# Scatters of a graph convolution released in groups of three chunks, and later one by one, by TensorE's progress

## The chip, the core and the metric

The kernel runs on one core of a Trainium2 chip. A core has TensorE (PE in the profile, its weight loads PEld), VectorE (DVE), ScalarE (ACT), GpSimd (POOL) and SyncE (SP), each with a queue that it works through in order; 16 DMA engines move data. The metric is the device time of one execution in microseconds (us). The kernel before takes 5031.5 us, the median of 3 runs (5031.15 to 5031.81).

## The reference

A layer of a graph network: 12500 nodes with 128 features, 412500 edges. Each edge takes a row of the normalised node table at `dst`, multiplies it with a filter made from its 20 attributes, and adds it to the row of `src`.

```python
h = jnp.maximum(_layernorm(x, axis=-1), 0.0)
h = h @ W_in2f
Wij = ssp(f_ij @ W_f1 + b_f1) @ W_f2 + b_f2      # ssp(x) = softplus(x) - log 2
Wij = Wij * rcut_ij[:, None]
x_ij = h[idx_j] * Wij                            # idx_j = dst, sorted
agg = jax.ops.segment_sum(x_ij, idx_i, num_segments=12500)   # idx_i = src, not sorted
out = x + ssp(agg @ W_o1 + b_o1) @ W_o2 + b_o2
```

## The kernel before

The edges are cut into 806 **chunks** of 512 (`CH`), a chunk into four **tiles** of 128 edges (`QT = 4`). `step(k)` (L1053) is called once for each chunk and writes out, in the order in which the engines are to work, what several chunks need at that moment; the schedule is manual, so each engine's queue is the order of the calls.

In step k TensorE does, in this order: the second half of the filter for chunk k+1 (`value`, tile `v`, L834), the rows of the node table for chunk k+2, selected by a one-hot product (`pick`, tile `picked`, L846), the count of places already taken for a later chunk (`rank`, tile `free`, L799 and L766), then for every second chunk the first half of the filter (`hidden`, tile `z`, L710). ScalarE scales `picked` to `hg` (L856) and sets up the next `v` (L826); VectorE reduces `free` to `top` (L771), from which come the places (`slot`), and multiplies `v` with `hg` to the messages `o` (`message`, L864).

Messages are summed in two stages. First each row of a message is written to a place of its own in a table `slots` in HBM, sorted by blocks of 128 nodes: this is the **scatter** (`Group.scatter`, L867), an indirect DMA on POOL's queue for each of the four tiles (L873, 128 rows of 516 bytes), so 3224 in all. Later, when all chunks of a segment of the edges are written, `Collect` reads the table back (`m`), makes one-hot matrices on VectorE (`to`, L932) and adds up on TensorE (`add`, tiles `acc` and `numbers`, L953). There are seven segments (`SEGS`, in groups of four chunks); the first has 352 chunks, so until chunk 369 (352 and `DELAY` = 17) TensorE has no collecting to do, and behind that the adds of a finished segment run at the end of each step, beside the chunks of the next.

Which order holds the scatters: a message is put on the list `waiting`, and the inner function `scatter` of `step` (L1072) takes chunks from it. From chunk 24 (`PACED`) on, and until 12 steps before the end, it does so at one point of step k alone: behind `value` of chunk k+1. It then issues the four scatters of chunk k-1, and the first of them is made to wait for the last matmul of that `v` (a semaphore of TensorE; "pace of TensorE"). The other three have no wait for TensorE. Every scatter waits for the landing of the scatter eight before it, and the first of a chunk for VectorE's message. In the other direction, `behind` (L595) makes matmuls wait for scatters 16 chunks back, and the buffers of `o` are 16 chunks deep (`BACK`).

```python
                if k + 1 not in vs:
                    vs[k + 1] = g.value(c, bs.pop(k + 1))
                    scatter(k, kept["v"])
```

Of the kernel before, what the change touches and what calls it, by code (L numbers as in the profile page):

```python
# [45 lines left out]
def gnn_kernel(  # L46
# [498 lines left out]
    with tc.tile_pool(name="edge", bufs=2) as edge, tc.tile_pool(  # L545
# [57 lines left out]
        class Group:  # L603
# [101 lines left out]
            def hidden(self, c):  # L705

                z = psum.tile([P, 2, CH], F32, name="z")
                for k in range(2):
                    rows = slice(32 * (c + k), 32 * (c + k) + RBF)
                    mm = nc.tensor.matmul(z[:, k, :], wf1[rows, :], self.f[rows, :],  # L710
                                          start=True, stop=True)
                    if k == 1:
                        behind(mm, self.g * NCHUNK + c - LZ, 3)
                self.pair[c] = z

            def hidden_log(self, c):
# [36 lines left out]
            def rank(self, c):  # L753

                seg = self.seg
                if c == 0:
                    self.top = edge.tile([P, TG], F32, name="top")
                    self.slot = edge.tile([P, TG], I32, name="slot", bufs=8)
                k = self.g * NCHUNK + c
                if k > seg.c0:  # L760
                    self.pass_on()
                if k == seg.cleared and k > seg.c0:
                    used = self.used()
                    self.limit(6 * len(segs), ALU.is_gt, seg.low, used[:, :, :NBLK - 1])
                    self.limit(6 * len(segs) + 1, ALU.is_gt, seg.low_last, used[:, :, NBLK - 1:])
                nc.tensor.matmul(free, after, self.inb[c], start=k == seg.c0, stop=False,  # L766
                                 skip_group_check=True)
                kept["inb"] = self.inb[c]

            def rank_end(self, c):  # L770
# [58 lines left out]
            def value(self, c, v):  # L829

                r = self.pair[c // 2 * 2][:, c % 2, :]
                k = self.g * NCHUNK + c - 1
                for i in range(QT):
                    mm = nc.tensor.matmul(v[:, i, :], r[:, i * P:(i + 1) * P], wf2,  # L834
                                          start=False, stop=True, skip_group_check=True)
                    if i == 1:
                        behind(mm, k, k % 2)
                kept["v"] = mm
                return v

            def pick(self, c, at, ps):
# [3 lines left out]
                for i in range(QT):  # L845
                    mm = nc.tensor.matmul(ps[:, i, :], at[:, i * P:(i + 1) * P], near,  # L846
                                          start=i == 0, stop=i == QT - 1, skip_group_check=True)
                    if i == 1:
                        behind(mm, k, 2 + k % 2)

            def picked(self, c, ps):

# [11 lines left out]
                nc.vector.tensor_mul(o[:, :, :P], v, hg)  # L864
                self.o[c] = o

            def scatter(self, c, after=None):  # L867

                views = self.seg.views
                o = self.o.pop(c)  # L870
                for i in range(QT):
                    j = c * QT + i
                    put = nc.gpsimd.indirect_dma_start(  # L873
                        out=views[j % VIEWS],
# [2 lines left out]
                        in_offset=None,  # L877
                    )
                    puts.append(put.ins.name)
                    if i == 0 and after is not None:  # L880
                        tc.add_manual_dep(
                            put.ins, after.ins.name,
                            mybir.DependencyInfo(mybir.DependencyClass.Sync,
# [10 lines left out]
        class Collect:  # L894
# [47 lines left out]
            def add(self, u):  # L942
                b0, nb, t0, nt = self.units[u]
                m, to = self.m.pop(u), self.to.pop(u)
                for j in range(nb * nt):
# [7 lines left out]
                    nc.tensor.matmul(self.acc[b // few][:, i, :], m[:, j, :P], to[:, j, :],  # L953
                                     start=t == 0, stop=t == self.seg.tiles(b) - 1)
# [94 lines left out]
        tops, ps = [], {}  # L1049
        waiting = []  # L1050
        LAG, PACED = 1, 24

        def step(k, units=()):  # L1053

# [11 lines left out]
            def message(k):  # L1066
                g, c = of(k)
                g.message(c, vs.pop(k), hgs.pop(k))
                waiting.append(k)
                scatter(k)  # L1070

            def scatter(k, after=None):  # L1072
                while waiting and (waiting[0] < PACED or k >= NCH - PACED // 2
                                   or after is not None and waiting[0] <= k - LAG):
                    j = waiting.pop(0)
                    g, c = of(j)
                    g.scatter(c, after if j >= PACED and k < NCH - PACED // 2 else None)

            if k in vs:
                message(k)  # L1080
# [369 lines left out]
```

## Time and profile before

| | |
|---|---|
| median of 3 runs | 5031.5 us |
| the profiled execution: time, span of its instructions | 5066.41 us, 5064.7 us |
| busy: PE, PEld, DVE, ACT, POOL | 3601.4, 2760.7, 3149.0, 2793.9, 3135.5 us |
| mean granted clock of TensorE | 0.784 |
| scatters (L873) | 3224, mean 959 ns each |

The profiled execution is 0.7% longer than the median of the others. No engine is busy for more than 71% of the span. "Granted clock" is the share of TensorE's clock that the throttle let through. In the trace's rows an idle time stands in brackets with what ended it: "issue" is a wait for nothing that the profile shows, "remote" one whose end came from a semaphore that it could not put down to an instruction. Of a scatter the trace shows how long POOL works on it (about 0.96 us); between two scatters that wait for nothing POOL always shows 0.30 us.

### The profile page before, as it was taken

To read this page: it belongs to the slowest core of one execution; us is meant where nothing else is said; L and a number is where in the kernel's file an instruction comes from. 1 tells how busy PE (TensorE), PEld (TensorE's weight loads), DVE (VectorE), ACT (ScalarE), POOL (GpSimd) and SP (SyncE) were. 2 spreads that over 40 slices of the span, in tenths; PEclk is the share of its full clock that TensorE was granted. 3 is DMA by queue.
4 is the path that set the end of the run, shared out by engine and by line. 5 is a ranking of instruction groups with operands and counts; after the bars stand their busy time and mean duration, and the time that the engine had idled before them with its cause. 6 is when DMAs were issued, how large, how long until landed. Compare 5 with 4: busy or idle time off the path is not lost. (4 is left out here: it accounts for less than half of the span.)

```text
span 5064.7 us, 68387 instructions
## 1 busy us (share of the span) xinstructions
PE 3601.4 (71%) x21594; PEld 2760.7 (55%) x21594; DVE 3149.0 (62%) x7192; ACT 2793.9 (55%) x5494; POOL 3135.5 (62%) x3298
## 2 busy tenths in 40 slices
PE   5666666566655565567777887887777787787778
PEld 3444444344433344356666666666666666666667
DVE  5565555555544454556666666666666676677767
ACT  5556566565555555555555555555555555555533
POOL 5566666666666666666666666666656666666553
PEclk7666666766666666679999888888988888888889
DMA  4555545445433334446657655567656765665658
GB/s 140 171 160 164 171 138 174 147 134 160 130 99 114 113 113 141 131 154 199 190 189 238 187 178 185 175 192 230 188 169 185 219 207 168 183 216 163 186 144 229
DMA packets 494767, 858.10 MB, mean 169 GB/s; under 512 B 141018, under 2 KB 276558, under 8 KB 494398
## 3 DMA queue, kind: packets, MB, share of 16 engines
q1 hardware_dynamic: 390798, 640.38, 42.3%
q0 software_dynamic: 103168, 213.15, 12.5%
q8 instruction: 174, 2.85, 0.2%
q14 instruction: 195, 1.60, 0.1%
q10 hardware_dynamic: 432, 0.13, 0.0%
HBM read 457.62 MB, written 395.69 MB: 168 GB/s over the span
## 5 line engine op out<-in xcount | busy, mean ns | idle before, releaser
L873 POOL DMA_INDIRECT slots<-o,slot x3224 | 3090.8, 959 | 1831.2 <-issue 808.9
L856 ACT ACTIVATE hg<-picked,rcut 128x128 f32<-128x128 f32 x3224 | 913.3, 366 | 1243.5 <-remote 356.7
L834 PEld LDWEIGHTS v<-wf,r 128*128 128x128 f32 x6448 | 1067.2, 247 | 324.2 <-issue 214.8
L834 PE MATMUL v<-wf,r 128*128 128x128 f32 x6448 | 1153.8, 335 | 73.4 <-issue 36.5
L864 DVE TENSOR_TENSOR o<-v,hg 128x512 f32<-128x512 f32 x806 | 553.0, 686 | 698.4 <-remote 207.0
L953 PEld LDWEIGHTS acc<-to,m 128*128 128x128 f32 x5660 | 782.1, 219 | 281.0 <-issue 144.0
L953 PE MATMUL acc<-to,m 128*128 128x128 f32 x5660 | 836.6, 308 | 117.1 <-DVE agg L987 45.2
L710 PE MATMUL z<-f,wf 20*128 20x512 f32 x1612 | 605.7, 826 | 355.7 <-issue 185.6
L771 DVE TENSOR_REDUCE top<-free 128x4 f32<-128x392 f32 x806 | 449.1, 557 | 602.2 <-remote 341.9
L932 DVE TENSOR_TENSOR to<-numbers,m 128x640 f32<-128x640 f32 (+3 forms) x793 | 630.4, 825 | 40.0 <-remote 12.0
L719 ACT ACTIVATE a<-z,bf 128x1024 f32<-128x1024 f32 x402 | 445.7, 1109 | 379.4 <-PE v L834 113.6
L747 DVE TENSOR_TENSOR inb<-numbers,blk 128x392 f16<-128x392 f32 x806 | 447.7, 556 | 297.3 <-PE picked L846 73.9
L846 PE MATMUL picked<-near,at 126*128 126x128 bf16 x3224 | 393.6, 248 | 330.2 <-issue 193.5
L799 PE MATMUL free<-inb,rest_of 128*128 128x392 f16 x806 | 318.1, 395 | 420.9 <-issue 277.2
L742 DVE SCALAR_TENSOR_TENSOR r<-z,nbf,a 128x1024 f32<-128x1024 f32 x402 | 513.5, 1277 | 127.9 <-ACT a L722 64.0
L826 ACT ACTIVATE v<-bf 128x512 f32<-128x512 f32 x806 | 486.6, 604 | 180.7 <-DVE o L864 72.5
L846 PEld LDWEIGHTS <-at 126*128 126x128 bf16 x3224 | 302.7, 114 | 389.7 <-issue 364.5
L953 PE MATMUL numbers<-to,m 128*128 128x128 f32 x2492 | 398.7, 324 | 121.0 <-DVE to L932 87.6
L953 PEld LDWEIGHTS numbers<-to,m 128*128 128x128 f32 x2492 | 367.5, 233 | 213.6 <-DVE to L932 136.6
L722 ACT ACTIVATE a<-a,half 128x1024 f32<-128x1024 f32 x402 | 461.5, 1148 | 13.1
L710 PEld LDWEIGHTS z<-f,wf 20*128 20x128 f32 x1612 | 152.4, 226 | 551.7 <-issue 303.0
L720 ACT ACTIVATE a<-a 128x1024 f32<-128x1024 f32 x402 | 424.9, 1057 | 12.8
(126 smaller groups left out, 1845.0 us busy)
## 6 DMA issues: line engine op xcount, KB each, us to landing
m<-slots SPq DMA_DIRECT2D x307, 387.0 KB
rel<-rel_d SPq DMA_DIRECT2D x202, 504.0 KB
m<-slots SPq DMA_DIRECT2D x278, 322.5 KB
f<-in_f_t SPq DMA_DIRECT2D x101, 512.0 KB
slots<-o,slot POOLq DMA_INDIRECT x3224
m<-slots SPq DMA_DIRECT2D x193, 258.0 KB
slots<-zero SPq DMA_DIRECT2D x96, 387.0 KB
slots<-zero SPq DMA_DIRECT2D x58, 516.0 KB
```

Of the source, the lines that this page charges most:

```text
L710: mm = nc.tensor.matmul(z[:, k, :], wf1[rows, :], self.f[rows, :], start=True, stop=True)
L722: nc.scalar.activation(a, a, AF.Ln, bias=half, scale=0.5)
L742: nc.vector.scalar_tensor_tensor(r, z, nbf1, a, op0=ALU.max, op1=ALU.add)
L771: nc.vector.tensor_reduce(self.top[:, c * QT:(c + 1) * QT], free_v, axis=mybir.AxisListType.X, op=ALU.max)
L826: nc.scalar.activation(v, spread(bf12, QT), AF.Copy)
L834: mm = nc.tensor.matmul(v[:, i, :], r[:, i * P:(i + 1) * P], wf2, start=False, stop=True, skip_group_check=True)
L846: mm = nc.tensor.matmul(ps[:, i, :], at[:, i * P:(i + 1) * P], near, start=i == 0, stop=i == QT - 1, skip_group_check=True)
L856: nc.scalar.activation(hg[:, i, :], ps[:, i, :], AF.Copy, scale=self.rcut[:, j:j + 1])
L864: nc.vector.tensor_mul(o[:, :, :P], v, hg)
L873: put = nc.gpsimd.indirect_dma_start(out=views[j % VIEWS], out_offset=bass.IndirectOffsetOnAxis(ap=self.slot[:, j:j + 1], axis=0), in_=o[: ...
L932: nc.vector.tensor_tensor(to[:, :n, :], count_ps[:, None, :].to_broadcast([P, n, P]), m[:, :n, P:].to_broadcast([P, n, P]), op=ALU.is_equal)
L953: nc.tensor.matmul(self.acc[b // few][:, i, :], m[:, j, :P], to[:, j, :], start=t == 0, stop=t == self.seg.tiles(b) - 1)
```

## The change

Instructions, their order on each engine and all buffers stay. What changes is for which matmul which scatter waits.

- `kept["mm"]` now holds TensorE's latest matmul, whichever it is, at each point of the program.
- The inner `scatter` is called at four points of a step: behind `value` ("v"), `pick` ("pick"), `rank` ("rank"), and at the step's end, behind `hidden` and the adds ("end").
- Chunks 24 to 368 (`j < LONE`, 352 + 17): only at "v", and only when three whole chunks are waiting. Their 12 scatters are issued together, and the first alone waits for TensorE: chunks j, j+1 and j+2 for `v` of chunk j+4. 
- Chunks 369 and up, until 12 steps before the end: at each of the four points one scatter, which waits for the latest matmul. So of chunk k-1 the first scatter waits for `v` of chunk k+1 as before, the second for `picked` of chunk k+2, the third for `free`, the fourth for the last add or `z` of step k.
- `Group.scatter` takes the tiles to be issued as an argument.

```diff
-            def scatter(self, c, after=None):
+            def scatter(self, c, tiles, after=None):
 
                 views = self.seg.views
-                o = self.o.pop(c)
-                for i in range(QT):
+                o = self.o[c] if tiles[-1] < QT - 1 else self.o.pop(c)
+                for i in tiles:
...
-                    if i == 0 and after is not None:
+                    if i == tiles[0] and after is not None:
...
+        LONE = segs[0].c1 + DELAY
...
-                waiting.append(k)
+                waiting.append((k, 0))
                 scatter(k)
 
-            def scatter(k, after=None):
-                while waiting and (waiting[0] < PACED or k >= NCH - PACED // 2
-                                   or after is not None and waiting[0] <= k - LAG):
-                    j = waiting.pop(0)
-                    g, c = of(j)
-                    g.scatter(c, after if j >= PACED and k < NCH - PACED // 2 else None)
+            def scatter(k, point=None):
+                while waiting:
+                    j, i = waiting[0]
+                    if j < PACED or k >= NCH - PACED // 2:
+                        n, after = QT - i, None
+                    else:
+                        where, n = ("v", 3 * QT) if j < LONE else ("each", 1)
+                        if point not in (("v", "pick", "rank", "end") if where == "each" else (where,)):
+                            return
+                        if j * QT + i + n > (k - LAG + 1) * QT:
+                            return
+                        after = kept["mm"]
+                    while n > 0:
+                        j, i = waiting.pop(0)
+                        g, c = of(j)
+                        e = min(QT, i + n)
+                        g.scatter(c, range(i, e), after)
+                        after = None
+                        n -= e - i
+                    if e < QT:
+                        waiting.insert(0, (j, e))
+                        return
...
-                    scatter(k, kept["v"])
+                    scatter(k, "v")
...
                 g.pick(c, ats.pop(k + 2), ps[k + 2])
+                scatter(k, "pick")
...
                 next(r, None)
                 tops.append(r)
+            scatter(k, "rank")
...
                     summed[0].add(summed[1])
                 summed[:] = c, u
+            scatter(k, "end")
```

POOL's queue in the first part, before: the four scatters of chunk 61, those of chunk 62, and the first of chunk 63. `PE_49` in the brackets is a wait for TensorE, `DVE_49` one for VectorE, `DMASW` one for an earlier scatter's landing; the numbers are those of buffers.

```order
L873 DMA slots0_116<-o_3273,slot_2930 206848x129 [waits DMASW4_49,DVE_49,PE_49]
L873 DMA slots0_116<-o_3273,slot_2930 206848x129 [waits DMASW5_49]
L873 DMA slots0_116<-o_3273,slot_2930 206848x129 [waits DMASW6_49]
L873 DMA slots0_116<-o_3273,slot_2930 206848x129 [waits DMASW7_49]
L873 DMA slots0_116<-o_3312,slot_2930 206848x129 [waits DMASW0_49,DVE_49,PE_49]
L873 DMA slots0_116<-o_3312,slot_2930 206848x129 [waits DMASW1_49]
L873 DMA slots0_116<-o_3312,slot_2930 206848x129 [waits DMASW2_49]
L873 DMA slots0_116<-o_3312,slot_2930 206848x129 [waits DMASW3_49]
L873 DMA slots0_116<-o_3353,slot_2930 206848x129 [waits DMASW4_49,DVE_49,PE_49]
```

The same place of POOL's queue in the changed kernel.

```order
L875 DMA slots0_116<-o_3273,slot_2930 206848x129 [waits DMASW4_49,DVE_49]
L875 DMA slots0_116<-o_3273,slot_2930 206848x129 [waits DMASW5_49]
L875 DMA slots0_116<-o_3273,slot_2930 206848x129 [waits DMASW6_49]
L875 DMA slots0_116<-o_3273,slot_2930 206848x129 [waits DMASW7_49]
L875 DMA slots0_116<-o_3308,slot_2930 206848x129 [waits DMASW0_49,DVE_49]
L875 DMA slots0_116<-o_3308,slot_2930 206848x129 [waits DMASW1_49]
L875 DMA slots0_116<-o_3308,slot_2930 206848x129 [waits DMASW2_49]
L875 DMA slots0_116<-o_3308,slot_2930 206848x129 [waits DMASW3_49]
L875 DMA slots0_116<-o_3345,slot_2930 206848x129 [waits DMASW4_49,DVE_49,PE_49]
```

Two of three waits for TensorE are gone; the scatters of a group of three chunks stand behind one.

POOL's queue in the second part, before: chunk 501, and the first scatter of chunk 502.

```order
L873 DMA slots1_117<-o_23643,slot_23303 116992x129 [waits DMASW4_49,DVE_49,PE_49]
L873 DMA slots1_117<-o_23643,slot_23303 116992x129 [waits DMASW5_49]
L873 DMA slots1_117<-o_23643,slot_23303 116992x129 [waits DMASW6_49]
L873 DMA slots1_117<-o_23643,slot_23303 116992x129 [waits DMASW7_49]
L873 DMA slots1_117<-o_23698,slot_23303 116992x129 [waits DMASW0_49,DVE_49,PE_49]
```

And there in the changed kernel.

```order
L875 DMA slots1_117<-o_23643,slot_23301 116992x129 [waits DMASW4_49,DVE_49,PE_49]
L875 DMA slots1_117<-o_23643,slot_23301 116992x129 [waits DMASW5_49,PE_49]
L875 DMA slots1_117<-o_23643,slot_23301 116992x129 [waits DMASW6_49,PE_49]
L875 DMA slots1_117<-o_23643,slot_23301 116992x129 [waits DMASW7_49,PE_49]
L875 DMA slots1_117<-o_23698,slot_23301 116992x129 [waits DMASW0_49,DVE_49,PE_49]
```

Every scatter now waits for TensorE, three more waits for each chunk, and nothing else moves.

TensorE's queue in a step of the second part, in the changed kernel (before, the rows are the same but for their line numbers, which are one or two lower): the four points lie behind `v`, behind the last `picked`, behind the second `free`, and behind the `acc`.

```order
L835 MATMUL v<-wf_63,r 128x128 x4
L847 LDWEIGHTS at
L847 MATMUL picked<-near,at 128x128
...
L800 LDWEIGHTS rest_of
L800 MATMUL free<-inb,rest_of 128x392
L767 LDWEIGHTS after
L767 MATMUL free<-inb,after 128x392
L710 MATMUL z<-f,wf_62 128x512 x2
L955 MATMUL acc<-to,m 128x128 x10
L835 MATMUL v<-wf_63,r 128x128 x4
```

Nothing moved here; the rows show where on TensorE the four points are.

More of the change, by code (lines that the diff above doesn't have):

```diff
@@ L713, in hidden @@
                         behind(mm, self.g * NCHUNK + c - LZ, 3)
+                kept["mm"] = mm
                 self.pair[c] = z
@@ L765, in rank @@
                     self.limit(6 * len(segs) + 1, ALU.is_gt, seg.low_last, used[:, :, NBLK - 1:])
-                nc.tensor.matmul(free, after, self.inb[c], start=k == seg.c0, stop=False,
-                                 skip_group_check=True)
+                kept["mm"] = nc.tensor.matmul(free, after, self.inb[c], start=k == seg.c0,
+                                              stop=False, skip_group_check=True)
                 kept["inb"] = self.inb[c]
@@ L837, in value @@
                         behind(mm, k, k % 2)
-                kept["v"] = mm
+                kept["mm"] = mm
                 return v
@@ L849, in pick @@
                         behind(mm, k, 2 + k % 2)
+                kept["mm"] = mm
             def picked(self, c, ps):
@@ L952, in add @@
                         self.acc[b // few] = self.room(b // few)
-                    nc.tensor.matmul(self.acc[b // few][:, i, :], m[:, j, :P], to[:, j, :],
-                                     start=t == 0, stop=t == self.seg.tiles(b) - 1)
+                    kept["mm"] = nc.tensor.matmul(
+                        self.acc[b // few][:, i, :], m[:, j, :P], to[:, j, :],
+                        start=t == 0, stop=t == self.seg.tiles(b) - 1)
                     if t == self.seg.tiles(b) - 1 and (i == few - 1 or b == NBLK - 1):
```

## The prediction

> **What bounds the kernel now.** I read the page first, then busy times by stage, then rows of POOL, TensorE and VectorE one under the other. The page:
>
> ```profile
> span 5064.7 us, 68387 instructions
> PE 3601.4 (71%) x21594; PEld 2760.7 (55%) x21594; DVE 3149.0 (62%) x7192; ACT 2793.9 (55%) x5494; POOL 3135.5 (62%) x3298
> PEclk7666666766666666679999888888988888888889
> L873 POOL DMA_INDIRECT slots<-o,slot x3224 | 3090.8, 959 | 1831.2 <-issue 808.9
> ```
>
> No engine is full, so the time goes in waits. The stages are cut at 178, 2211 and 4828 us, where chunks 24 and 369 and the unpaced end begin; the columns are the stretch, busy us and count for PE, PEld, DVE, ACT and POOL, then granted clock, DMA share, GB/s. Below them are the messages that fall into the two stages.
>
> ```profile
> 178.00:2211.00 2033.00, 1237.87 (x5779) 836.26 (x5778) 1090.36 (x2782) 1188.51 (x2354) 1316.83 (x1373) 0.66 0.45 141
> 2211.00:4828.00 2617.00, 2068.90 (x13975) 1685.83 (x13973) 1794.92 (x3802) 1424.57 (x2807) 1625.23 (x1697) 0.87 0.62 192
> ...
> L864 DVE TENSOR_TENSOR o<-v,hg x345: 672/691/693, 182.5 to 2209.9; 128x512 f32<-128x512 f32 x173
> ...
> L864 DVE TENSOR_TENSOR o<-v,hg x424: 674/683/695, 2212.6 to 4826.9; 128x512 f32<-128x512 f32 x142
> ```
>
> A chunk takes 2033 / 345 = 5.89 us in the first stage and 2617 / 424 = 6.17 us in the second. POOL's four scatters take 4 x (0.96 + 0.30) = 5.04 us of either, so POOL is nearest to full, and idles 0.85 and 1.13 us for each chunk. Why it idles is seen in one group of the first stage: POOL's first, last and next scatter, TensorE's matmuls in between, and VectorE's reduction that waits for `free`.
>
> ```profile
> 1260.80 0.97 POOL L873 DMA_INDIRECT slots<-o,slot  x1 [2.77 <-PE free L766]
> ...
> 1274.73 0.96 POOL L873 DMA_INDIRECT slots<-o,slot  x1 [0.30 <-issue]
> 1278.21 0.95 POOL L873 DMA_INDIRECT slots<-o,slot  x1 [2.52 <-remote]
> ...
> 1268.87 0.53 PE L766 MATMUL free<-inb,after 128*128 128x392 f16 x1
> 1269.20 1.33 PE L834 MATMUL v<-wf,r 128*128 128x128 f32 x8
> 1278.50 0.48 PE L799 MATMUL free<-inb,rest_of 128*128 128x392 f16 x1 [7.58 <-DVE top L771]
> ...
> 1277.88 0.57 DVE L771 TENSOR_REDUCE top<-free 128x4 f32<-128x392 f32 x1 [7.39 <-remote]
> ```
>
> `free` ended at 1269.40, yet VectorE starts on it at 1277.88; `v` ended at 1270.53, yet POOL's next scatter starts at 1278.21. Both come a good two us after POOL's last scatter ended (1275.69). So **TensorE's announcements do not get through while POOL scatters back to back**: they are let go when POOL has stopped. VectorE, ScalarE and TensorE stand still for seven us, and POOL itself then waits for a `v` that is long done. The same in the second stage, with runs of four and of eight scatters (first, last, next), and TensorE's rows beside the run of four:
>
> ```profile
> 2988.39 0.96 POOL L873 DMA_INDIRECT slots<-o,slot  x1 [2.67 <-PE picked L846]
> ...
> 2992.18 0.96 POOL L873 DMA_INDIRECT slots<-o,slot  x1 [0.30 <-issue]
> 2994.37 0.96 POOL L873 DMA_INDIRECT slots<-o,slot  x1 [1.23 <-PE acc L953]
> ...
> 2844.71 0.96 POOL L873 DMA_INDIRECT slots<-o,slot  x1 [2.10 <-PE free L766]
> ...
> 2853.56 0.96 POOL L873 DMA_INDIRECT slots<-o,slot  x1 [0.30 <-issue]
> 2856.71 0.96 POOL L873 DMA_INDIRECT slots<-o,slot  x1 [2.19 <-PE free L766]
> ...
> 2989.66 1.38 PE L953 MATMUL acc<-to,m 128*128 128x128 f32 x10
> 2990.88 1.06 PE L834 MATMUL v<-wf,r 128*128 128x128 f32 x8
> 2991.77 0.39 PE L846 MATMUL picked<-near,at 126*128 126x128 bf16 x4
> 2992.16 0.33 PE L766 MATMUL free<-inb,after 128*128 128x392 f16 x1
> ```
>
> From one run's start to the next: 5.98 us for 4, 12.00 for 8, 17.41 for 12 scatters, so 1.50, 1.50 and 1.45 us a scatter. The pause grows with the run (1.23, 2.19, 2.52); length hardly matters. A chunk costs 5.8 to 6.0 us in this way as long as `v` is done in time, and the kernel stands close above it: 5.89 and 6.17.
>
> What lies above it in the second stage are pauses in which `v` truly comes late:
>
> ```profile
> 2928.31 0.95 POOL L873 DMA_INDIRECT slots<-o,slot  x1 [0.31 <-issue]
> 2932.36 0.96 POOL L873 DMA_INDIRECT slots<-o,slot  x1 [3.09 <-PE picked L846]
> ...
> 2927.44 2.93 PE L953 MATMUL acc<-to,m 128*128 128x128 f32 x12
> 2930.16 1.92 PE L834 MATMUL v<-wf,r 128*128 128x128 f32 x8
> 2932.36 0.33 PE L766 MATMUL free<-inb,after 128*128 128x392 f16 x1
> ```
>
> **First stage, chunks 24 to 368.** The change takes 230 of 345 waits for TensorE off POOL, so runs of 12 become the rule; before, they stand among runs of 4 and 8. The price of a group is read where two runs of 12 follow each other:
>
> ```profile
> 1451.19 0.96 POOL L873 DMA_INDIRECT slots<-o,slot  x1 [2.46 <-PE picked L846]
> ...
> 1468.59 0.95 POOL L873 DMA_INDIRECT slots<-o,slot  x1 [2.54 <-PE v L834]
> ...
> 1486.43 0.96 POOL L873 DMA_INDIRECT slots<-o,slot  x1 [2.99 <-PE v L834]
> ```
>
> Two groups in 35.24 us, 17.6 each. 115 groups x 17.6 = 2024 us against 2033: a gain of 9 us, if the awaited `v` is ready when POOL stops. It should be: the last `v` of the run at 1260.80 had ended 5.2 us before POOL did. That the scatters come up to two chunks later delays nobody: the matmuls that wait for scatters wait for those 16 chunks back, over 90 us at 5.89 a chunk. The two waits taken away per group cost nothing in themselves: POOL's 0.30 us stands before scatters with and without.
>
> TensorE will stand still in every group for seven us, as at 1278.50. The clock granted in this stage is 0.66 already; were it 0.50 throughout, TensorE's 1237.87 / 345 = 3.59 us of work a chunk would become 4.74, and 14.2 for three, still under 17.6. The Trainium skill (TensorE: Matmul & The Clock Gate, "Why this matters for your kernels") says the same against this stage: idle gaps of more than about 3 us drop the clock to half. By it TensorE would be cold for most of each group, and the sum stays as above, since 14.2 is under 17.6; the row of 0.66 agrees with it.
>
> **Second stage, chunks 369 to 792.** Each scatter gets a wait, three more for each chunk, 1272 in all. A wait that is already met costs nothing (the 0.30 us again; every scatter's landing wait is of this kind). One that is not met costs a pause. Behind it on POOL's queue are only more scatters, and for those nobody waits for 16 chunks; VectorE, ScalarE and TensorE feel POOL only through the held announcements. What a single scatter holds back no row shows, since all runs are of 4, 8 or 12. From below: nothing, 1.26 us from one to the next; from above: as long as a run of four does, 0.96 + 1.23 = 2.19 us. I take the 1.5 us a scatter that 4 and 8 agree on, being nearest.
>
> The four points are not spread evenly: in the step at 2989.66 the adds end at 2991.04, `v` at 2991.94, `picked` at 2992.16, `free` at 2992.49, four points in 1.45 us. So once one scatter has run, the waits of the next three are mostly met, and the four go as they do today, one scatter shifted: the last of a chunk goes at the end of the adds, ahead of `v`. Where `v` is late that is a gain: the adds of the late step ended at 2930.37, 1.71 us before `v` at 2932.08, so one scatter (1.26 us) fits into what was pause. All of today's excess is 6.17 - 6.00 = 0.17 us a chunk. One scatter in four leaves the pause, so about a quarter to a third of it goes: 0.05 us x 424 = 21 us. From above the gain is bounded by 0.17 x 424 = 72 us, unless TensorE itself gets faster (third rival).
>
> Ahead of chunk 24 and in the last 237 us nothing changes. Sum: -9 - 21 = -30 us on the profiled execution's 5066.41, 0.6%; on the median of 5031.5 that is 5001 us.
>
> **Rivals.** *A second pause in each step (slower).* The scatter that goes at the end of the adds holds back `v`, `picked` and `free` in their turn, POOL has run out of met waits, and pauses before the next three. Price: at 1.50 us for a run of one, 0.24 us more than the 1.26 of today's back-to-back scatters, and up to 0.93 (1.23 - 0.30) if it holds as long as a run of four; 0.4 us in half of the steps is 85 us, less 9 of the first stage: 5107. It decides when the added pauses exceed the 0.05 us saved, that is, when more than about one step in eight has one. For it: the four points span 1.45 us, about as long as one scatter holds. Against it: a POOL that falls behind finds all its waits met.
>
> *`v` late in the first stage (slower).* With no pause at 4 or 8, TensorE gets its answers later, and a `v` that misses the release costs what the late one above cost, 3.09 - 1.23 = 1.86 us. In one group of three that is 38 x 1.86 = 71 us, and the time about 5080. Against it: 5.2 us of reserve.
>
> *TensorE freed (much faster).* If no announcement is held longer than one scatter, VectorE and ScalarE answer at once, and the second stage goes at 1.45 us a scatter, 5.80 a chunk: 0.37 x 424 = 157 us and 9: 4865.
>
> *No effect.* Runs of 4 and 8 form again out of met waits, and the first stage stays as it is: 5031. The Trainium skill speaks for this: SBUF — State Buffer, "SBUF: two separate sides", has it that a DMA and a compute instruction cannot slow each other, but for GpSimd and VectorE at their shared port. By it when scatters go would not matter to TensorE at all. The row of `top` at 1277.88 speaks against it.
>
> **How the numbers follow.** Forecast 0.38 (5001, its own range 4960 to 5025), second pause 0.26 (5107), late `v` 0.10 (5080), TensorE freed 0.14 (4865), no effect 0.12 (5031). 0.2%, or 10 us, is what can be told from no change. Faster: 0.36 of the forecast and 0.14; within 0.2%: 0.12 and the forecast's last 0.02; slower: 0.26 and 0.10. The range reaches from 4900, which leaves out most of the freed case, to 5120, which leaves out those second pauses that cost more than 0.4 us in half of the steps.
>
> **What would show it.** In the first stage POOL's rows should show a pause after every 12 scatters and at no other place, of 2.5 to 3 us, and the next run 17.4 to 17.8 us after the last; pauses over 3.5 us mean that `v` is late. The second stage is decided by its length (2617 us now) and by runs shorter than four: single scatters with pauses on both sides, and a stage longer than 2617, mean the second pause. The freed case would show in waits of `hg` and `top` for TensorE that shrink, and in a granted clock above 0.87. Wrong in both directions would be the forecast if single scatters hold announcements far shorter or longer than 1.5 us.

## The result and the profile after

The kernel takes 5050.05 us after the change (5045.73 to 5055.21, 5 runs) against 5031.15 before (5026.58 to 5031.81, 5 runs): a ratio of 1.0041 with a 95% interval of 1.0028 to 1.0054, 19 us slower. 5001 was forecast. The profiled execution of after took 5052.65 us. Its page:

```profile
span 5050.9 us, 69659 instructions
PE 3592.7 (71%) x21594; PEld 2756.4 (55%) x21594; DVE 3158.7 (63%) x7192; ACT 2787.6 (55%) x5494; POOL 3145.6 (62%) x3298
PEclk7666666666666666668899898889888988888879
L875 POOL DMA_INDIRECT slots<-o,slot x3224 | 3100.7, 962 | 1797.2 <-issue 778.8
```

No engine's busy time has grown by more than 10 us, and none is full. The stages, cut again where chunks 24 and 369 and the unpaced end begin (after, busy times by stretch):

```profile
173.00:2223.00 2050.00, 1235.86 (x5776) 834.82 (x5776) 1092.39 (x2781) 1185.30 (x2349) 1315.13 (x1368) 0.66 0.45 139
2223.00:4803.00 2580.00, 2054.93 (x13971) 1677.98 (x13969) 1801.60 (x3800) 1419.76 (x2809) 1635.61 (x1702) 0.88 0.64 195
```

The first stage takes 2050 us where the profile before showed 2033 and the forecast said 2024; the second 2580, where 2617 stood and 2596 was forecast. So the first stage lost time and the second gained some. Two groups of the first stage, one clean and one not (after, POOL's first and last scatter of each group, and the first of the group behind):

```profile
841.17 0.96 POOL L875 DMA_INDIRECT slots<-o,slot  x1 [2.69 <-remote]
...
855.08 0.96 POOL L875 DMA_INDIRECT slots<-o,slot  x1 [0.31 <-issue]
858.63 0.97 POOL L875 DMA_INDIRECT slots<-o,slot  x1 [2.59 <-remote]
...
872.57 0.96 POOL L875 DMA_INDIRECT slots<-o,slot  x1 [0.30 <-issue]
880.32 0.96 POOL L875 DMA_INDIRECT slots<-o,slot  x1 [6.79 <-PE v L835]
```

The first group costs 17.46 us, as priced; the second 21.69, since POOL stops at 873.53 and then waits 6.79 us for `v`. TensorE, ScalarE and one row of VectorE in that group, after:

```profile
866.37 0.53 PE L767 MATMUL free<-inb,after 128*128 128x392 f16 x1
866.70 1.91 PE L373 MATMUL hps<-win,xT 128*128 128x128 f32 x8
868.41 1.09 PE L835 MATMUL v<-wf,r 128*128 128x128 f32 x8
...
873.59 2.08 PE L710 MATMUL z<-f,wf 20*128 20x512 f32 x4 [0.78 <-issue]
877.96 2.08 PE L835 MATMUL v<-wf,r 128*128 128x128 f32 x8 [2.29 <-ACT v L827]
```

```profile
871.38 0.57 DVE L772 TENSOR_REDUCE top<-free 128x4 f32<-128x392 f32 x1 [4.76 <-issue]
...
875.64 0.60 ACT L375 ACTIVATE hb<-hps 128x512 bf16<-128x512 f32 x1 [5.92 <-PE z L710]
876.14 1.14 ACT L858 ACTIVATE hg<-picked,rcut 128x128 f32<-128x128 f32 x4
877.31 0.60 ACT L827 ACTIVATE v<-bf 128x512 f32<-128x512 f32 x1
```

`hps` (rows of the node table that TensorE makes in between) ended at 868.61, but ScalarE stands idle for 5.92 us and starts on it at 875.64, 2.1 us after POOL stopped. Behind it in ScalarE's queue are `hg` and the start of the next `v`; so the `v` that POOL waits for begins only at 877.96. This announcement was held to the end of the run, and what POOL waits for depends on it: the release comes first, and then a chain of 4.4 us more. The trace's own records of TensorE's semaphore show the release: none between 865.84 and 875.62, then six within 0.28 us.

Not every announcement is held that long. `free` ended at 866.90, and VectorE took it up at 871.38, 4.5 us late but with POOL in the middle of its run. In the profile before, 55 of the 94 times that VectorE stood idle for over half a microsecond ahead of `top` in the first stage ended like this, while POOL was still scattering, and 65 of 67 in the second. So the sentence of the prediction that announcements do not get through while POOL scatters back to back is too strong: they come through microseconds late, some within the run and the rest behind it.

Over all 114 groups of the first stage the awaited `v` ended after POOL had stopped in 36; the pause is 2.55 us in the median and over 3.2 us in 18. In each of these 18 POOL starts again 0.28 us after `v` has ended, so it is `v` that it waits for. The cycle of a group is 17.45 us in the median and 17.88 in the mean: 0.43 x 114, some 50 us, lies in the late ones.

In the second stage shorter runs have appeared, as meant (after, first scatter of each of several runs):

```profile
2271.13 0.96 POOL L875 DMA_INDIRECT slots<-o,slot  x1 [1.54 <-PE picked L847]
...
2279.93 0.96 POOL L875 DMA_INDIRECT slots<-o,slot  x1 [1.51 <-PE numbers L955]
...
2283.01 1.06 POOL L875 DMA_INDIRECT slots<-o,slot  x1 [0.86 <-PE free L767]
...
2292.57 0.96 POOL L875 DMA_INDIRECT slots<-o,slot  x1 [0.70 <-PE acc L955]
2294.95 0.96 POOL L875 DMA_INDIRECT slots<-o,slot  x1 [1.42 <-PE picked L847]
```

A run of six takes 8.80 us here, and the lone scatter at 2292.57 holds POOL for 2.38 us up to the next one. Over the stage runs of 4, 5, 7 and 8 cost 6.00, 7.40, 10.42 and 11.85 us in the median, 1.48 to 1.50 a scatter; only 25 scatters of 1696 stand alone, at 2.00 us in the mean.

### The profile page after: what moved, and what is told of

It reads as the page before. It is cut to its first block, busy times and chain, and to the rows that moved or that the text cites. A ratio compares the mean times of both kernels' runs of the same rounds, so it can differ in the third digit from the quotient of the medians.

```text
span 5050.9 us, 69659 instructions
## 1 busy us (share of the span) xinstructions
PE 3592.7 (71%) x21594; PEld 2756.4 (55%) x21594; DVE 3158.7 (63%) x7192; ACT 2787.6 (55%) x5494; POOL 3145.6 (62%) x3298
## 5 line engine op out<-in xcount | busy, mean ns | idle before, releaser
L955 PEld LDWEIGHTS acc<-to,m 128*128 128x128 f32 x5660 | 794.5, 221 | 291.2 <-issue 168.4
L955 PE MATMUL acc<-to,m 128*128 128x128 f32 x5660 | 850.5, 311 | 127.8 <-issue 51.4
```

Of the source, the lines that this page charges most:

```text
L955: kept["mm"] = nc.tensor.matmul(self.acc[b // few][:, i, :], m[:, j, :P], to[:, j, :], start=t == 0, stop=t == self.seg.tiles(b) - 1)
```

## The experiments

**Two kinds of chip.** The runs come from several chips (which one the first comparison used is not on record), and they fall into two kinds: in five comparisons, the first among them, the kernel before takes 5026 to 5072 us, and in three, on three chips, 4202 to 4209 us. Ratios and differences are always to the kernel before on the same chip. The theory at the start: the first part (three chunks behind one `v`) loses through late `v`, the second (a wait at each scatter) gains a little. The rival: the first part gains, and the single waits of the second part lose. The first part alone, as a change of after:

```diff
-                        where, n = ("v", 3 * QT) if j < LONE else ("each", 1)
+                        where, n = ("v", 3 * QT) if j < LONE else ("v", QT)
```

> Only the groups of three chunks up to chunk 368; behind that the scatters of a chunk wait for v as before. Theory (late v in the first stage): 15 to 25 us slower than before, first stage about 2049 us as in the changed kernel. Rival (the second stage's single waits cost it): 5 to 10 us faster than before.

The second part alone:

```diff
-                        where, n = ("v", 3 * QT) if j < LONE else ("each", 1)
+                        where, n = ("v", QT) if j < LONE else ("each", 1)
```

> Only the single waits behind chunk 368; up to there the scatters of a chunk wait for v as before. Theory (late v in the first stage): within 10 us of before or up to 30 us faster. Rival (a second pause in each step): 20 to 30 us slower than before, with many runs of one scatter.

With them the kernel before was profiled twice more:

> The kernel before, for a second profile, since the one shown took 5066.41 us and its median 5031. If the profiled execution was an odd one, its second stage (chunks 369 to 792, 2617 us there) comes out some 30 us shorter here and its first stage (2033 us) the same; the first part of the change then loses and the second gains little or nothing. If 2617 us is typical, the second part of the change gains 36 us, and something of equal size must be lost where no profile shows it.

> The kernel before once more, for a third profile: as before_again.

The four ran on a chip where the kernel before takes 4202.3 us (21 runs). First part alone: 4203.04 us, ratio 1.0000 (0.9991 to 1.0009). Second part alone: 4201.13, ratio 0.9998 (0.9989 to 1.0007). The kernel before took 4207.68 and 4203.72 under the profile. The first part's result is neither theory's; the second's lies within the 10 us of its theory, but so does no effect at all. The kernel before had become 16% shorter in its first stage and 18% in its second, so nothing on its odd profile could be told from it. So the whole change was run on another such chip, with the first part again, and with a measurement of what bounds that kernel: in before, every second chunk's last scatter issued twice.

> The changed kernel, unaltered, beside the kernel before on the same chip. The first two experiments came from a chip on which the kernel before takes 4202 us and TensorE's announcements are not held while POOL scatters. Theory: the change can only act where they are held. If the kernel before takes about 4200 us here as well, the changed kernel takes the same, within 5 us; if it takes about 5030 us, the changed kernel is 10 to 30 us slower, as in the first comparison. Rival (the change acts through something else, such as the 1272 added waits on POOL): slower by 10 to 30 us on either kind of chip.

> The first stage's part of the change alone (three chunks of scatters behind one v), beside the whole change on the same chip. If announcements are held here (the kernel before at about 5030 us): theory, the first stage gives back its 17 us through late v, so 10 to 20 us slower than before, and some 30 of 115 pauses over 3.2 us; rival, the first stage saves its 9 us and what was lost lies in the second stage and the tail, so 5 to 15 us faster. If they are not held (4200 us): within 5 us of before.

```diff
+                    if i == QT - 1 and (self.g * NCHUNK + c) % 2 == 0 and 24 < self.g * NCHUNK + c < 793:
+                        put = nc.gpsimd.indirect_dma_start(
...
                     puts.append(put.ins.name)
```

> The kernel before with the last scatter of every second chunk from 26 on issued twice (same rows, same addresses, 384 scatters more), so that the price of one scatter is measured by itself. Where announcements are held, theory: each costs what a run costs a scatter, 1.45 to 1.50 us, so 557 to 576 us more; rival (POOL's own time sets the pace): 1.26 us each, 485 us more. Where they are not held, both say 1.26 us each or a little less, 450 to 485 us, if POOL is the bound there; less than 300 us if it is not.

The whole change: 4201.11 us against 4202.1, ratio 0.9998 (0.9989 to 1.0008). The first part: 4200.26, ratio 0.9996 (0.9987 to 1.0005). Lines of the whole change's page and its stages on this chip (the third row is VectorE's copy that waits for a buffer of `o`):

```profile
span 4200.0 us, 69659 instructions
L858 ACT ACTIVATE hg<-picked,rcut 128x128 f32<-128x128 f32 x3224 | 912.4, 365 | 423.6 <-PE picked L847 413.9
L865 DVE COPY o<-place 128x4 f32<-128x4 f32 x806 | 157.2, 195 | 679.5 <-DMA slots<-o,slot 678.3
```

```profile
130.00:1833.00 1703.00, 1166.42 (x5784) 793.96 (x5782) 1088.82 (x2784) 1187.33 (x2360) 1292.48 (x1345) 0.71 0.54 167
1833.00:3993.00 2160.00, 1868.15 (x14008) 1551.41 (x14007) 1784.49 (x3806) 1415.49 (x2809) 1638.92 (x1709) 0.93 0.77 233
```

and the row of `hg` from the page of after on the first chip:

```profile
L858 ACT ACTIVATE hg<-picked,rcut 128x128 f32<-128x128 f32 x3224 | 915.7, 366 | 1397.4 <-remote 429.5
```

ScalarE idles 424 us before `hg` instead of 1397, and nearly all of that ends with `picked` itself, where the largest share was "remote" before: here TensorE's announcements are not held. A chunk takes 1703 / 345 = 4.94 us in the first stage and 2160 / 424 = 5.09 in the second (cut at POOL's scatters instead of the messages, 5.06 in both), about 4 x 1.26: POOL scatters without a pause, is itself the bound, and lags so far behind the messages that its waits for TensorE are long met. VectorE waits for scatters to land (679.5 us) before it may write the next `o`. The doubled scatters bear that out. That kernel took 5753.54 us in its single execution, 1551 more, far over the 485 expected, since each of the 384 copies waited for the scatter that it repeats (its row on the page):

```profile
L880 POOL DMA_INDIRECT slots<-o,slot x384 | 367.7, 957 | 1187.0 <-DMA slots<-o,slot 1036.6
```

367.7 + 1187.0 = 1555 us on POOL, and 1551 more for the kernel: each microsecond that POOL spends is one of the end's. The price of a plain scatter was not got from it.

A third chip of this kind gave the same for three kernels, among them one with the second part's waits in both stages:

> The second stage's part alone: a wait at each scatter from chunk 369 on, the pacing of before ahead of it. Where announcements are held (kernel before at about 5030 us), theory: the prediction's second term was right, 15 to 35 us faster, since the first stage's part alone cost 46 us where the whole cost 19, and the second stage's length falls from about 2609 (the run with the first part alone) to about 2580. Rival (the second pause of the prediction): 0 to 80 us slower, and the first part's loss was smaller in the first comparison. Not held (4200 us): within 5 us.

```diff
-                        where, n = ("v", 3 * QT) if j < LONE else ("each", 1)
+                        where, n = ("each", 1)
```

> The second stage's pacing in both stages: every scatter from chunk 24 on waits for a quarter of TensorE's step. Held: theory, what helps is that POOL stops where TensorE has something to announce, so the first stage gains as well and the kernel is 25 to 60 us faster than before; rival (in the first stage TensorE stands still for lack of answers, and the points of a step come too close together there): no better than with the second part alone, or slower than before by up to 40 us. Not held: within 5 us.

> The changed kernel beside its parts on one chip. Held: theory, the parts add up, 10 to 30 us slower than before (46 from the first part, less 15 to 35 from the second); rival, they don't add, and it is over 35 us slower or not slower at all. Not held: within 5 us.

Before 4208.5; second part 4209.51 (ratio 0.9999, 0.9989 to 1.0008), waits everywhere 4209.03 (0.9999, 0.9990 to 1.0008), the whole change 4208.53 (0.9997, 0.9988 to 1.0006). The 1272 added waits cost nothing that can be measured (the intervals leave some 5 us), and where nothing is held the change is without effect.

**The first part where announcements are held.** A chip with the kernel before at 5027.1 us ran the first part and, as a change of before, a kernel whose scatters wait for TensorE nowhere:

> The first stage's part alone once more, in search of the conditions of the first comparison (kernel before at 5031 us, announcements held). Theory there: late v in about 36 of 115 groups makes the first stage 10 to 20 us longer, 5041 to 5051. Rival there: the 9 us are saved and the loss lies behind chunk 369: 5016 to 5026. On a chip at 4200 us: within 5 us of before.

```diff
-        LAG, PACED = 1, 24
+        LAG, PACED = 1, 100000
```

> The kernel before with no scatter waiting for TensorE at all. On a chip at 4200 us, theory (POOL's own time is the bound and its waits are met anyway): the same within 5 us; rival (the pacing earns something by itself): 10 us or more apart. On a chip at 5031 us, theory (a scatter costs 1.45 to 1.50 us however they are grouped): within 30 us of before; rival (without pauses TensorE, VectorE and ScalarE get their answers only when POOL runs dry): 100 us or more slower.

The first part alone takes 5073.52 us, ratio 1.0109 (1.0089 to 1.0128): 46 us slower by the medians (45 to 64 by the interval), over twice the loss of the whole and well over the theory's 10 to 20. Without any pacing it is 5253.96, ratio 1.0459 (1.0438 to 1.0481), 227 us slower: the rival's side. POOL in that kernel:

```profile
1301.97 0.96 POOL L873 DMA_INDIRECT slots<-o,slot  x1 [3.18 <-DVE o L864]
...
1320.90 0.96 POOL L873 DMA_INDIRECT slots<-o,slot  x1 [0.30 <-issue]
1325.72 0.96 POOL L873 DMA_INDIRECT slots<-o,slot  x1 [3.85 <-DVE o L864]
```

Here it runs 16 scatters and then has to wait for the next message itself (23.75 us from run to run, 1.48 a scatter). Its commonest run in the first stage is one of 12 and costs 18.09 us in the median, where the first part alone has 17.42; in the second stage runs of 8 cost 12.51 where that kernel has 11.87. So a scatter does not cost the same however they are grouped: without a stop at the right moment the other engines have not done their part when POOL runs dry.

**The second part where announcements are held.** On a chip with before at 5028.34 us:

> The second stage's part alone, in search of a chip on which announcements are held (kernel before at about 5030 us). There, theory: the prediction's second term was right, 15 to 35 us faster, since the first part alone cost 46 us where the whole cost 19; second stage near 2580 us, first stage 2000 to 2010 us. Rival (the second pause of the prediction): 0 to 80 us slower. At 4200 us: within 5 us.

> The second stage's pacing in both stages. Held: theory, what helps is that POOL stops where TensorE has something to announce, so the first stage gains as well and the kernel is 25 to 60 us faster than before; rival (in the first stage the points of a step lie too close together): no better than with the second part alone, or up to 40 us slower than before. At 4200 us: within 5 us.

The second part alone: 5004.58 us, ratio 0.9952 (0.9938 to 0.9966), 24 us faster; 15 to 35 were expected. Waits at each scatter in both stages: 4993.13, ratio 0.9934 (0.9920 to 0.9947), 35 us faster, in the range of its theory; 11 of them come on top of the second part alone, and its profiled first stage is 1998 us where that of the second part alone is 2007. This kernel beats both, and equals them on the other kind of chip. Stages of the second part alone:

```profile
177.00:2184.00 2007.00, 1228.87 (x5764) 828.87 (x5763) 1086.13 (x2781) 1185.95 (x2349) 1318.02 (x1370) 0.66 0.46 142
2184.00:4755.00 2571.00, 2047.05 (x13986) 1675.38 (x13983) 1799.50 (x3802) 1421.18 (x2810) 1634.38 (x1700) 0.88 0.64 195
```

and of the first part alone, on its chip:

```profile
178.00:2214.00 2036.00, 1237.79 (x5766) 838.92 (x5765) 1091.29 (x2781) 1184.10 (x2350) 1309.71 (x1362) 0.66 0.45 140
2214.00:4823.00 2609.00, 2050.47 (x13987) 1671.96 (x13988) 1792.04 (x3801) 1427.77 (x2810) 1641.18 (x1707) 0.88 0.63 193
```

With the old pacing the first stage takes 2007 us, with groups of twelve 2036. With the old pacing the second takes 2609, with a wait at each scatter 2571. (Two chips, with the kernel before at nearly the same time.) These 29 and 38 us are not the 46 and 24 of the medians, since a cut at the message of chunk 369 leaves waiting scatters of the groups to the second stage. Cut at POOL's scatters, chunk 369's first one starts 39.6 us later with groups of twelve (2239.1 against 2199.5), and from there to chunk 793 the second part saves 27.6 (2567.3 against 2594.9). Groups of twelve had 15 of 114 pauses over 3.2 us there, not the 30 expected, and a mean cycle of 17.81 over a median of 17.42: 0.39 x 114 = 45 us.

**Why `v` is late.** Two theories: it is awaited too early in TensorE's course (phase), or TensorE is held so much in an unbroken run that it does not do three steps a group (rate). Against each other: groups of twelve that wait for the `v` of the step before, and groups of eight; the old pacing behind chunk 369 in both.

```diff
                 kept["mm"] = mm
+                kept["older"], kept["newer"] = kept.get("newer"), mm
                 return v
...
-                        after = kept["mm"]
+                        after = kept["older"] if j < LONE else kept["mm"]
```

> The first stage's part alone (groups of twelve scatters, one wait each), but the wait is for the v of the step before, which ended a step earlier; behind chunk 369 the pacing of before. Held (kernel before at about 5030 us): theory A (the loss of 46 us is a matter of phase: the awaited v misses the release by up to 7.5 us in one group of three): with a step's reserve the late pauses go, first stage 2000 to 2010 us, the kernel within 15 us of before. Theory B (a matter of rate: in an unbroken run of twelve TensorE gets its answers only now and then and does not do three steps a group): late pauses stay, or come as waits for the message instead, first stage 2030 us or more, the kernel 30 to 60 us slower. Not held (4200 us): within 5 us.

```diff
-                        where, n = ("v", 3 * QT) if j < LONE else ("each", 1)
+                        where, n = ("v", 2 * QT) if j < LONE else ("v", QT)
```

> In the first stage eight scatters (two chunks) behind one v instead of twelve, behind chunk 369 the pacing of before. Held: theory A and B both expect less loss than the 46 us of twelve; A (a late v costs a pause, more often tried): 10 to 40 us slower; B (what counts is how long POOL runs without a stop that it could make earlier): 5 to 25 us slower; rival (the loss has nothing to do with the length of a run): 46 us slower again. Not held: within 5 us.

Before 5025.63 there. The older `v`: 5045.14, ratio 1.0036 (1.0024 to 1.0048), 20 us slower. Groups of eight: 5037.72, ratio 1.0023 (1.0010 to 1.0036), 12 us slower. The loss with groups of eight lies in the ranges of both theories and is smaller than the 46 us of twelve on another chip, which speaks against the rival; but POOL did not keep to eight there: it went on to 16 in 35 of its 138 runs, the next `v` being done already. With the older `v` the loss lies between what the two theories said. That both have a share is not shown, for the step of reserve did not last: the awaited `v` ended 2.44 us before POOL's stop in the median, where it was 2.66 in after, and late in 26 of 114 groups, where it was 36. When POOL stopped, TensorE had in most groups finished `v` up to chunk j+3 instead of j+4 (j being POOL's next chunk): it was one chunk less ahead. That speaks for the rate. With the older `v`, 11 of 114 pauses are over 3.2 us and the first stage stands at 2027:

```profile
177.00:2204.00 2027.00, 1256.39 (x5765) 852.72 (x5763) 1087.43 (x2782) 1187.14 (x2355) 1315.64 (x1371) 0.66 0.45 141
```

One thing was seen and not tried: the work at L373 (`hps`) falls whole into 20 of the 114 runs of twelve, and these have 9 of the 18 long pauses in after and 8 of the 15 in the first part alone. With the older `v` none of the runs that hold it whole has one, but in 7 of that kernel's 11 long pauses TensorE does this work in the pause itself. So this extra work goes with half of the long pauses or more; that it causes them, no run without it shows.

**Whether the parts add, and the profile of before.** In a fifth comparison of the held kind, on a chip of its own (before 5071.56 us):

> The changed kernel once more, for whether its parts add. Held (kernel before at about 5030 us): the first part alone cost 46 us, the second alone gained 24, so theory (they add): 15 to 30 us slower than before, first stage 2036 to 2050 us, second 2570 to 2585. Rival (they act on each other, the 19 us of the first comparison belong to that chip): under 10 or over 40 us slower. Not held: within 5 us.

> The kernel before, profiled again, since the prediction's profile was of an execution 35 us over the median. Held, theory: that execution's excess lay in both stages, so that here the first takes 2005 to 2012 us (as in the run with the second part alone) and the second 2595 to 2605; rival (the stages were typical and the excess lay elsewhere): 2033 and 2617 again. Not held: 1700 and 2150.

The whole change: 5110.75, ratio 1.0077 (1.0054 to 1.0101), 39 us slower; theory had 15 to 30, the rival over 40, so neither. The kernel before: 5067.78. Stages of before, then of after, on this chip:

```profile
176.00:2204.00 2028.00, 1219.31 (x5775) 822.95 (x5776) 1089.50 (x2782) 1189.75 (x2356) 1321.56 (x1373) 0.67 0.45 141
2204.00:4819.00 2615.00, 2062.86 (x13982) 1675.51 (x13982) 1795.26 (x3801) 1427.33 (x2807) 1630.79 (x1697) 0.88 0.62 192
```

```profile
177.00:2267.00 2090.00, 1244.98 (x5779) 846.66 (x5779) 1090.98 (x2782) 1184.63 (x2354) 1315.79 (x1369) 0.66 0.44 137
2267.00:4877.00 2610.00, 2081.04 (x13969) 1704.73 (x13968) 1800.26 (x3800) 1418.20 (x2806) 1634.05 (x1700) 0.87 0.64 192
```

The first part costs 62 us here and the second gains 5. But the profiled execution of after is the slowest of its six, some 20 us over their median, and that of before 4 us under the median there, so these 57 us are more than the 39 of the medians. The signs are those of the parts alone; the sizes differ from chip to chip, and why the second part gained 24 us on one chip and 5 on another stays open. These stages of before (2028 and 2615) stand close to those of the prediction's profile (2033 and 2617), and so do its runs of 4, 8 and 12 scatters (6.08, 12.00 and 17.52 us in the median, 6.08, 12.01 and 17.53 there; with the first part alone, 6.01 and 11.87 for 4 and 8). So the prediction's profile looks like one from a chip of this sort, and the runs of 5031 us like those of the others; that it was so is not shown.

## Why the prediction was wrong

**What bounds the kernel** was read rightly in the main for the comparisons in which announcements are held: a scatter costs 1.45 to 1.50 us in a run, and pauses end with a release some 2 us after POOL stops. That nothing gets through before that was read from one group of scatters and is wrong. That all this holds on some chips only, no view of one trace could tell.

**First stage, -9 us: the step that failed.** The price of a group was right: 17.6 said, 17.42 to 17.62 measured in the median. What failed is "if the awaited v is ready when POOL stops. It should be". It was late in 36 of 114 groups, and the mean group cost 17.81 to 18.19 us. The reserve of 5.2 us was read from one run of twelve of the kernel before, and that is a selected case: there each chunk had its own wait, so POOL came to twelve in a row only when `v` was on time twice on the way. Within that selection 5.2 us is typical: of the 70 runs of twelve in that stage `v` was late behind one, with 5.15 us to spare in the median. But 88 of the stage's 159 runs had stopped after 4 or 8 scatters, and behind the 43 runs of four `v` was late in 24. The change took exactly those stops away, and to spare are 2.66 us in the median. It was also another `v`: that of two chunks past POOL's next one, where the change awaits that of four past. Measured by itself the term is +46 us.

Part of it was the base: 2024 us for 115 groups was set against the 2033 of one execution, while the old pacing takes 2007 us on a chip with before at 5028. Against that a median group (115 x 17.45 = 2007) gains nothing, and the 78 groups without a late `v` alone (17.37 in the mean, 1998 for 115) would gain about the 9 us: runs of 4, 8 and 12 cost nearly the same a scatter, as the prediction itself had found.

**Second stage, -21 us: borne out on one chip.** -24 us alone, with 15 to 35 expected. A lone scatter was priced too low (1.5 us said; 2.00 in the mean and 2.38 in the row above, over the upper bound of 2.19), but only 25 of 1696 stand alone in after, so the price hardly enters. What the argument rested on, that late pauses shrink when one scatter goes ahead of them, fits POOL's pauses: beyond 0.30 us each they take 449 us in the second stage with the old pacing (first part alone) and 421 with the new (second part alone), 28 us less, though POOL stops more often (0.81 times a chunk, 0.64 before); those over 2.5 us fall from 31 to 10.

**The rivals.** *`v` late in the first stage* is what happened, at the place and nearly at the rate (one group in three) that the rival gave; it had a chance of 0.10, and its 71 us were more than the 46 measured, so that its 5080 us came out 30 too long. *A second pause in each step*: its deciding point was passed (0.17 more stops a chunk, more than one step in eight), and still the stage did not become longer, since a stop behind a short run is short (1.05 to 1.46 us in the median behind runs of one to four, 2.04 behind eight). *TensorE freed*: no; the clock stays at 0.66 and 0.88. *No effect* is right in the time on the three chips where nothing is held, but not by its mechanism: runs of 4 and 8 do not form again there, POOL hardly stops at all. The Trainium skill (SBUF — State Buffer, "SBUF: two separate sides") has it that the ports of the engines and those of the DMAs cannot contend with each other, and that contention arises only at the port that GpSimd and VectorE share and among what comes through the DMAs' own ports; those three chips fit it, and in the other comparisons the row of `hps` (held for 7 us) and the 227 us that the missing pacing costs speak against its being the whole of it.

**What would show it** had the sign right: pauses over 3.5 us meant a late `v`, and there are 17 of them in after. That 5050 us lies between 4900 and 5120 owes nothing to the forecast's own path, whose range ended at 5025.

## What to carry to other kernels

A wait that looks redundant in the trace may be the moment at which another engine's answers get through: look not only at the runs without it but at those that it cut short, for they are where the engine it waits for was late. The longest run seen under the old rule is a selected sample and gives no reserve for a rule that makes all runs long. And before a gain under one per cent is worked out against a profile's stage, see that this execution's time is that of the runs it will be compared with.

## What the runs showed of the hardware

The same program takes 4202 to 4209 us on three chips and 5026 to 5072 in the other five comparisons, 20% apart, with POOL's scatters 0.96 us each on both. What differs is when semaphores change. A count over the traces' records: of the 3224 x 16 = 51584 increments with which the scatters' landings are reported, the kernel before left 51277 records on a chip at 4202 us and 10718 to 10945 in its two profiles on the other kind (after: 51341 and 11422). The engines' own increments show the same: of VectorE's 6529, ScalarE's 3051 and TensorE's 4062, a chip at 4202 us left 6507, 3043 and 4045 records, the profile before 3034, 1464 and 3452. The Trainium skill (DMA: Bandwidth & Descriptors, "Why a DMA increments its semaphore by 16 and not by 1") has each of 16 engines report its share of such a DMA by one increment; the first number agrees, and in the second most increments have no record of their own. That fits announcements which come through in bunches on the second kind, those of the DMA engines, VectorE and ScalarE as well as TensorE's; but a missing record is no proof, since the `free` that VectorE took up at 871.38 left none either. Whether the chips themselves differ, or something that is set up on them, or whether the recording of the executions plays a part, no run here shows; nor was it tried to provoke the one kind on the other. What holds the announcements back stays open.
